# Two products of nothing per pass ahead of the experts, one of them outside the planner's account

## The chip, the cores and the metric

The kernel runs on one core of a Trainium2 chip. The metric is the device time of one execution in microseconds (us); lower is better. A core has five engines that run side by side, each in the order of its own instruction stream: TensorE (PE in the profile; its weight loads are listed as PEld), VectorE (DVE), ScalarE (ACT), GpSimd (POOL) and SyncE (SP), which here issues the transfers. They wait for one another on semaphores. TensorE's clock is granted by a throttle and can be halved for a time; the profile shows what was granted.

## What is computed

Four layers in a row over `x` of 8 sequences, 512 tokens and 128 features, each added to `x` behind a layer norm: a state-space block (a convolution, a scan over the tokens with decay), a mixture of eight experts, a local attention with 16 heads, and the same mixture again.

```python
x = L0_attn_a_x
x = x + _L0_attn_a_ref(_layernorm(x, axis=-1), L0_attn_a_W_in, ...)
x = x + _L0_ffn_ref(_layernorm(x, axis=-1), L0_ffn_w_router, ...)
x = x + _L0_attn_b_ref(_layernorm(x, axis=-1), L0_attn_b_Wq, ...)
x = x + _L0_ffn_ref(_layernorm(x, axis=-1), L0_ffn_w_router, ...)
```

The mixture is dense: every token goes through all eight experts, which are weighted afterwards.

```python
g = jnp.einsum('bsh,ehf->ebsf', x, w_gate)
u = jnp.einsum('bsh,ehf->ebsf', x, w_up)
h = jax.nn.silu(g) * u
expert_out = jnp.einsum('ebsf,efh->ebsh', h, w_down)
...
out = jnp.einsum('ebsh,bse->bsh', expert_out, cw)
```

## The kernel before

Features lie on the 128 partitions, the 512 tokens of a sequence along the free side. Products that need precision are three products of split operands (a high part and a low remainder, `matmul3`). The experts are one long stream, `ffn_stream`: for each of two layers, eight sequences, eight experts and four slices of the hidden width it issues three products for the gate (`g`), three for the up projection (`u`) and, some slices later, three for the down projection (`y`). Between them ACT takes silu of `g`, DVE multiplies by `u`, and two engines split the result `h` into high and low parts. The first sequence of the first layer is done in halves of 256 tokens. State-space and attention work of other sequences is put in beside this stream.

The order of the work is not left to the hardware nor written out by hand. While the program is built, a planner keeps an account of time. `Clock` holds for each engine the end of its last instruction, and books a cost for each new one (`cost`, and `product` for PE). `Engine` wraps a hardware engine: a call on `pe`, `act`, `dve`, `pool` or `sp` issues the real instruction and books it. The work is written as generators in `Lanes`; `tick` gives the next step to the one that can start soonest by the account. What comes out is one fixed order of instructions for each engine. A call on `nc.tensor`, `nc.vector` or another raw engine issues an instruction that the account never hears of.

Before the first experts the front of sequence 0 has to be done: its layer norm (`x_m`, `xn_m`), transposes (`tp_m`), the input projection (`mh`), the convolution (`mv`), the products for step and state inputs (`mde`, `mbc`), spreads of the rows over partitions (`mbx`, `mcx`), the decays (`mdec`) and scans (`mst`), the output products (`mo`), then the experts' layer norm (`xn_f`), transposes (`tp_f`) and the router (`lps_f`, `rps_f`, `cps_f`). All this is short work that goes from engine to engine, on two halves of 256 tokens (`first_halves`). Meanwhile ACT and POOL split the experts' weights (`wg`, `wu`, `wd`) into high and low parts.

During this front the build runs the loop that the change touches, lines 1747 to 1757. `warm` is an accumulator tile of one bank, 128 by 512. Each time no lane has anything to start (`lanes.tick()` did nothing) and the account is past `WARM` = 3.5 us, it issues one product of nothing on PE: weights `sel[:, 0]` (128 by 128), moving operand 256 columns of `sel`, result into the left half of `warm`. Nobody reads that result. The call books its cost by `product`, and the loop then adds 0.1 us to PE's end. It stops when the first half of the experts' input is planned to be there; the bank is freed by `freed(e)`. All warm products write the same tile.

Later, `keep_warm` (line 1766) issues similar products into a bank of their own, tile `idle`, where the experts' stream waits. The change leaves them as they are.

In the profile nearly all instructions carry line 269, the one line of `Engine` that issues them, so they are told apart by the names of their tiles. `warm<-sel` are the products of nothing.

Of the kernel before, what the change touches and what calls it, by code (L numbers as in the profile page):

```python
# [18 lines left out]
P = 128  # L19
B, L, DIM = 8, 512, 128  # L20
NT = L // P
HALF = L // 2
# [355 lines left out]
def block_kernel(ctx: ExitStack, tc: tile.TileContext, x, pack_a, pack_b, pack_c, w_qkv, mask, mask_t, w_o,  # L378
                 w_gate, w_up, w_down, out):
    nc = tc.nc  # L380
# [40 lines left out]
    def take(who, shapes, names):  # L421
        held[who] += len(shapes)
        del lanes.free["bank"][: len(shapes)]
        return [ps.tile(shape, F32, tag="s", name=name) for shape, name in zip(shapes, names)]
# [6 lines left out]
    def side(shape, name):  # L431
        return (yield from sides((shape, name)))[0]

    def freed(t, who="others"):

        held[who] -= 1
        lanes.give("bank", t + TO_PE)
        return t
# [9 lines left out]
    def load_x(b, i, tag):  # L448

        yield from lanes.take("x")  # L450
        if i:
            yield "S", done[b, i]
        t = lnp.tile([P, NT, DIM], F32, tag="x", name=f"x_{tag}", bufs=NX)
        e = sp.dma_start(out=t, in_=xs[b, i].rearrange("(t p) d -> p t d", p=P))
        return t, e
# [6 lines left out]
    def now(gen):  # L462

        try:
            next(gen)
        except StopIteration as stop:
            return stop.value
        raise AssertionError("no buffer is free")
# [636 lines left out]
    def ffn_preps():  # L1105
        for s in range(1, 2 * B):
            k, b = divmod(s, B)
            turn["prep"] = s
            yield lambda: (b, 2 * k + 1) in done and pos[0] >= s - LEAD
            xc = yield from load_x(b, 2 * k + 1, f"f{k}_{b}")  # L1110
            yield from ffn_prep(k, b, xc)
# [291 lines left out]
    def attention_preps():  # L1403
        yield lambda: "weights" in done
        consts = yield from attention_consts()
        for b in range(B):
            yield lambda: (b, 2) in done and (b < 2 or ("heads", b - 2) in done)
            yield from attention_prep(b, consts)
# [310 lines left out]
    with mctx:  # L1719
        sb = msb  # L1720
        mc = {}

        def late(part):
            return lambda: pos[0] >= turn[part] - MAMBA_DUE

        def fronts(seqs):
            for b in seqs:
                turn["front"] = b
                xc = first_x
                if b:  # L1730
                    xc = yield from load_x(b, 0, f"m{b}")
                    yield lambda: ("front", b - 1) in done
                yield from mamba_front(b, sb, mc, xc)
                done["front", b] = 0.0

        def backs(seqs):
            for b in seqs:
                turn["back"] = b
                yield lambda: b in handed and (b - 1, 1) in done
                yield from mamba_back(b, sb, mc, lambda gen: lanes.add(gen, due=late("back")))  # L1740

        first(fronts(range(1)))
        first(mamba_consts(sb, mc))
        lanes.add(ffn_weights(sb))
        clock.hold = INF

        warm = now(side([P, L], "warm"))
        while (0, 0) not in ready or ready[0, 0][1] == 0:
            if lanes.tick():
                continue  # L1750
            if clock.now > WARM:
                sel = mc["sel"]
                e = pe.matmul(warm[:, :HALF], sel[:, 0], sel[:, : HALF // P], start=True, stop=True)
                clock.end["T"] += 0.1
            else:
                clock.now += 0.03
        freed(e)

        done["first"] = 0.0
        lanes.add(backs(range(1, B)), due=late("back"))  # L1760
        lanes.add(fronts(range(1, B)), due=late("front"))
        lanes.add(ffn_preps(), rank=0, due=lambda: pos[0] >= turn["prep"] - PREP_DUE)
        lanes.add(attention_preps(), rank=QRANK, joins=JOIN_ATT)
        stream = ffn_stream()

        def keep_warm():

            if pos[0] < WARM_TO and clock.now > clock.end["T"] + WARM_GAP and lanes.are_free("bank"):
                t, = take("experts", [[P, L]], ["idle"])
                sel = mc["sel"]  # L1770
                freed(pe.matmul(t[:, :HALF], sel[:, 0], sel[:, : HALF // P], start=True, stop=True), "experts")

        while "weights" not in done or (B - 1, 1) not in done:
            if next(stream):
                lanes.idle()
                keep_warm()
            else:
                lanes.tick()
# [63 lines left out]
def build(arrays):  # L1842
    import concourse.bacc as bacc

    nc = bacc.Bacc("TRN2", target_bir_lowering=False, num_devices=1)
    args = [
        nc.dram_tensor(name, a.shape, mybir.dt.from_np(a.dtype), kind="ExternalInput").ap()
        for name, a in arrays.items()
    ]
    args.append(nc.dram_tensor("out", (B, L, DIM), F32, kind="ExternalOutput").ap())  # L1850
    with tile.TileContext(nc) as tc:
        block_kernel(tc, *args)
    return nc
# [10 lines left out]
```

## Time and profile before

| | us |
|---|---|
| median of 3 runs | 1352.26 |
| lowest and highest | 1350.01 and 1354.05 |
| the profiled execution | 1351.71 |
| its span, first to last instruction | 1349.9 |
| PE busy, share of the span | 1328.8, 98% |
| warm products on PE, busy | 17.9 (111 of them) |
| first warm product, last warm product | 2.3 and 32.8 |
| first product of the experts (`g`) | 34.25 |

Times in the trace count from the start of the span. The timeline lists, for each engine, runs of like instructions with start and length and, in brackets, how long the engine had stood idle before them and what ended that idle time. The length of a product is longer than the distance from one to the next, since products overlap in PE's pipeline; so the distance between starts (the pitch) is what a further product costs, not its length.

### The profile page before, as it was taken

The page shows a single profiled execution, that of the slowest core. Times are in us where ns is not written, and L with a number is a line of the kernel's source. Part 1 is how long each engine was busy: PE and PEld are TensorE (multiplying, and loading weights), DVE is VectorE, ACT ScalarE, POOL GpSimd, SP SyncE. Part 2 cuts the span into 40 slices and gives each one's busy share as a digit, 9 for nine tenths or more (in the row PEclk, how much of TensorE's full clock was granted, in tenths as well). Part 3 has the DMA queues.
Part 4 walks back from the last instruction along what each step waited for, and adds up shares of the span by engine and source line. Part 5 has one row for each costly group of instructions (what it writes and reads, how often), then busy time and mean ns, then how long its engine had stood idle before and what let it go on. Part 6 is the DMA issues. An engine that isn't in the chain of part 4 may idle for free.

```text
span 1349.9 us, 29483 instructions
## 1 busy us (share of the span) xinstructions
PE 1328.8 (98%) x10261; PEld 1053.4 (78%) x10261; DVE 1038.5 (77%) x3114; ACT 964.2 (71%) x1694; POOL 941.4 (70%) x1042
## 2 busy tenths in 40 slices
PE   7999999999999999999999999999999999999998
PEld 7877778788788877777777777777777777778886
DVE  6887888688888877897788887888888787845443
ACT  7768576867787556776777777777877767765654
POOL 5877576776767757676766767767677676777776
PEclk9999999999999999999999999999999999999999
DMA  4320303232111261344344453344443434121111
GB/s 126 95 82 28 87 24 101 64 80 76 42 48 56 63 86 52 72 102 113 79 102 114 98 125 88 95 110 102 104 99 96 114 76 102 47 71 53 40 40 40
DMA packets 182204, 107.74 MB, mean 80 GB/s; under 512 B 86401, under 2 KB 162088, under 8 KB 182056
## 3 DMA queue, kind: packets, MB, share of 16 engines
q1 hardware_dynamic: 182056, 105.87, 31.6%
q8 instruction: 81, 1.33, 0.4%
q14 instruction: 67, 0.55, 0.1%
HBM read 77.64 MB, written 27.79 MB: 78 GB/s over the span
## 4 chain that ended last, share of the span: by engine, by line
PE 91%; ACT 2%; issue 2%; POOL 2%; DVE 1%; POOLq 0%; DVEq 0%
PE u L269 26%; PE g L269 25%; PE y L269 25%; PE ao L269 2%; PE aw L269 2%; PE as L269 2%; PE mo L269 1%; POOL h L269 1%; PE aqk L269 1%; ACT h L269 1%; DVE h L269 1%; PE aout L269 1%; PE mde L269 1%; PE yp L269 1%; PE tp_f L269 0%
## 5 line engine op out<-in xcount | busy, mean ns | idle before, releaser
L269 POOL TENSOR_TENSOR h<-h,h 128x512 fp32r<-128x512 f32 x492 | 639.8, 1309 | 280.0 <-ACT h L269 223.2
L269 PE MATMUL u<-xt_f,wu 128*128 128x512 f32 (+1 forms) x1584 | 451.4, 395 | 3.6 <-ACT h L269 2.7
L269 PE MATMUL g<-xt_f,wg 128*128 128x512 f32 (+1 forms) x1584 | 448.4, 393 | 2.1 <-ACT h L269 1.9
L269 PE MATMUL y<-h,wd 128*128 128x512 f32 (+1 forms) x1584 | 445.6, 392 | 1.4 <-POOL h L269 0.8
L269 DVE TENSOR_TENSOR h<-u,h 128x512 f32<-128x512 f32 x420 | 285.8, 686 | 157.7 <-PE u L269 109.8
L269 ACT ACTIVATE h<-g 128x512 f32<-128x512 f32 x512 | 303.4, 597 | 124.8 <-PE g L269 100.6
L269 ACT CAST h<-h 128x512 fp32r<-128x512 f32 x437 | 268.3, 618 | 169.2 <-DVE h L269 167.6
L269 PEld LDWEIGHTS g<-xt_f,wg 128*128 128x128 f32 x1584 | 288.5, 189 | 70.2 <-ACT h L269 3.0
L269 PEld LDWEIGHTS y<-h,wd 128*128 128x128 f32 x1584 | 288.3, 188 | 70.3 <-POOL h L269 1.5
L269 PEld LDWEIGHTS u<-xt_f,wu 128*128 128x128 f32 x1584 | 286.7, 189 | 71.5 <-ACT h L269 4.1
L269 POOL TENSOR_TENSOR acc<-acc,cwb 128x512 f32<-128x512 f32 (+1 forms) x114 | 148.0, 1298 | 52.1 <-DVE cwb L269 44.9
L269 ACT ACT_TABLE_LOAD x109 | 139.8, 1283 | 25.2 <-PE g L269 23.7
L269 DVE CUSTOM_DVE_ANT_0 amasked<-as,maskq 128x60 f32<-128x60 f32 x640 | 95.3, 213 | 4.9 <-PE as L269 4.6
L269 DVE TENSOR_TENSOR cwb<-y,cwb 128x512 f32<-128x512 f32 (+1 forms) x116 | 77.4, 668 | 14.1 <-PE y L269 13.6
L269 DVE TENSOR_TENSOR apt<-aw,maskk 125x400 f32<-125x400 f32 (+2 forms) x160 | 88.1, 570 | 0.0
L269 DVE SCALAR_TENSOR_TENSOR h<-h,g 128x512 f32<-128x512 f32 x92 | 62.3, 681 | 28.3 <-ACT h L269 27.8
L269 ACT ACTIVATE apt<-apt 125x400 f32<-125x400 f32 (+2 forms) x160 | 81.5, 540 | 0.4
L269 DVE SCALAR_TENSOR_TENSOR h<-u,h 128x512 f32<-128x512 f32 x92 | 62.5, 683 | 3.3 <-PE g L269 0.5
L269 DVE DVE_READ_ACCUMULATOR2_ANT amx<- 128x1 f32 x640 | 51.9, 81 | 0.0
L269 DVE CAST h<-h 128x512 fp32r<-128x512 f32 x75 | 50.6, 675 | 1.2
L269 DVE COPY v<-avr 125x128 f32<-125x128 f32 (+2 forms) x40 | 25.5, 638 | 26.5 <-PE ao L269 26.0
L269 PEld LDWEIGHTS ao<-apt,v 125*32 125x32 f32 (+2 forms) x1280 | 27.4, 109 | 14.6 <-DVE h L269 4.0
(205 smaller groups left out, 1241.4 us busy)
## 6 DMA issues: line engine op xcount, KB each, us to landing
cwb<-cwd_f SPq DMA_DIRECT2D x124, 256.0 KB
aqd<-apc SPq DMA_DIRECT2D x32, 192.0 KB
ks<-aqd SPq DMA_DIRECT2D x48, 93.8 KB
x_fo<-x SPq DMA_DIRECT2D x16, 256.0 KB
aqd<-apc SPq DMA_DIRECT2D x32, 128.0 KB
x_f<-x SPq DMA_DIRECT2D x15, 256.0 KB
qs<-aqd SPq DMA_DIRECT2D x48, 75.0 KB
aod<-aos SPq DMA_DIRECT2D x24, 100.0 KB
```

What stands on the lines that cost most here:

```text
L269: f(*args, **kw)
```

## The change

Each pass of the loop issues a second product of nothing. It has the same weights and the same moving operand and writes the right half of `warm`. It is issued on the raw engine, so the account doesn't book it: the planned order of all else is the same.

```diff
             if clock.now > WARM:
                 sel = mc["sel"]
                 e = pe.matmul(warm[:, :HALF], sel[:, 0], sel[:, : HALF // P], start=True, stop=True)
+
+                nc.tensor.matmul(warm[:, HALF:], sel[:, 0], sel[:, : HALF // P], start=True, stop=True)
                 clock.end["T"] += 0.1
             else:
                 clock.now += 0.03
```

## The prediction

> **What bounds the kernel now.** I read the page first: its engine shares and the chain of waits, to see which engine sets the end.
>
> ```profile
> span 1349.9 us, 29483 instructions
> ...
> PE 1328.8 (98%) x10261; PEld 1053.4 (78%) x10261; DVE 1038.5 (77%) x3114; ACT 964.2 (71%) x1694; POOL 941.4 (70%) x1042
> ...
> PE 91%; ACT 2%; issue 2%; POOL 2%; DVE 1%; POOLq 0%; DVEq 0%
> ```
>
> TensorE (PE) is occupied for 98% of the span and carries 91% of the chain that ended last. Almost nothing behind the first 34 us can swallow a late start; whatever PE starts late there, it ends late. So the question is how much later the experts (products g, u, y) begin. Next I read the products of nothing by their tile, and PE's occupied time in the stretches they fill (columns: stretch, us, busy us and count).
>
> ```profile
> L269 PE MATMUL warm<-sel x111: 274/283/579, 2.3 to 32.8; 128*128 128x256 f32 x111
> ...
> 9.72:11.19 1.47, 1.47 (x11) 1.27 (x10) 1.00 1.07 369
> 23.92:24.56 0.64, 0.64 (x3) 0.55 (x3) 0.50 0.00 0
> 28.34:31.34 3.00, 3.00 (x23) 2.79 (x23) 1.00 0.00 0
> ```
>
> There are 111 of them, from 2.3 to 32.8 us. Their pitch at full clock: eleven take 1.47 us, of which the last one's own length is 0.28, so (1.47 - 0.28) / 10 = 0.12 us. At the half clock (the 0.50 column) three take 0.64, 0.21 each. The build's account books 0.22 for each pass of the loop (256 / 2245 + 0.003, and 0.1 on top), so it has long reckoned with PE later than it was; but what counts is the order that came of it, and that the trace shows these runs without a gap between two products.
>
> Third, PE's waits ahead of 34 us and behind it (columns: us in total, times, longest).
>
> ```profile
> PE mbx L269 <- DVE mst L269: 2.6, 1, 2.6
> PE warm L269 <- POOL sel L269: 2.3, 1, 2.3
> PE mbc L269 <- ACT mxb L269: 1.8, 1, 1.8
> PE tp_f L269 <- DVE xn_f L269: 0.4, 1, 0.4
> PE mbx L269 <- DVE mbc L269: 0.2, 1, 0.2
> ...
> PE rps_f L269 <- DVE mcx L269: 0.2, 1, 0.2
> ```
>
> The 2.3 us are the start of PE's work, ahead of every product of nothing. The other five are all the room there is: 5.2 us, four of them ahead of the experts' start, the fifth at 37.5 us.
>
> Last, the clock by stretches (columns: us, then busy time and count of PE, PEld, DVE, ACT, POOL, then granted clock, DMA).
>
> ```profile
> 9.38:12.79 3.41, 1.81 (x12) 1.56 (x12) 2.83 (x5) 2.67 (x7) 3.13 (x4) 1.00 1.09 366
> 19.62:23.03 3.41, 1.13 (x10) 0.93 (x8) 2.59 (x6) 3.31 (x9) 0.00 (x0) 1.00 0.00 0
> 23.03:26.44 3.41, 3.11 (x14) 3.12 (x15) 3.24 (x7) 3.29 (x8) 0.12 (x1) 0.50 0.00 0
> 67.40:70.82 3.42, 2.27 (x8) 1.19 (x8) 3.39 (x11) 3.37 (x5) 0.95 (x2) 1.00 0.01 2
> 70.82:74.23 3.41, 3.41 (x15) 3.02 (x15) 2.50 (x8) 3.40 (x8) 2.65 (x5) 0.50 0.26 77
> 173.22:176.63 3.41, 1.49 (x7) 0.87 (x6) 1.25 (x3) 3.38 (x6) 2.37 (x2) 1.00 0.21 72
> 176.63:180.04 3.41, 3.40 (x8) 2.75 (x9) 2.48 (x4) 2.17 (x4) 1.75 (x2) 0.50 0.01 5
> ```
>
> Three times the clock is halved for 3.41 us, each time behind a stretch of that length with few products in it. These stretches cost up to 1.7 us each (half of 3.41).
>
> **The change, part by part.** Nothing is removed or moved. 111 products are added, each behind its twin: same weights, same 256 columns, the other half of the same accumulator tile, so the pitch of the twin is the nearest row: 0.12 us, taken. Its ends: 0.11 (the pitch of the 128-column mo products at full clock, eight in 1.05 us) and 0.21 (half clock). Nothing cheaper: PE runs its stream in order. The account doesn't see them, so the order of all engines stays. No DMA, no instruction of another engine and no queue is touched. Added work: 111 x 0.12 = 13.3 us on PE.
>
> What of it shows is followed from product to product. "Late" is against before; at each step the later of "PE free" and "operand there" decides.
>
> - wdt_ps, before at 6.39: 19 more products. The first 19 took 4.12 us, about sixteen at 0.21 and the rest at 0.12, so the full clock came at 5.96, where the grid of 3.41 us of the clock rows puts it too. It comes then either way, so the 19 more run at 0.12: late 2.3.
> - tp_m, 7.38: 4 more, late 2.8 (PE). mh, 8.76: 8 more, late 3.7 (PE; its operand, by ACT's and DVE's casts behind tp_m, is late 2.8). mh's third product waited for DVE until 9.38 and no longer does: mh ends at 13.3, late 3.4.
> - ACT's mv, 10.27: before, mh had ended at 9.88 and ACT was still at wxz until 10.25. Now it starts as mh ends, 13.4: late 3.1. This carries on by DVE and ACT to mxb.
> - mbc, 12.99: PE is free at 11.03 + 3.5 + 11 x 0.12 = 15.85, mxb is there at 16.0. Late 3.1, by its operand; the wait of 1.8 is nearly filled.
> - mbx, 15.10: 6 more. PE free at 18.6, operand at 18.2: late 3.5 (PE). From here ACT and DVE (tanh, exponentials, clips, scan mst) run late by 3.5, set by mde just behind.
> - mbx of the second half, 19.41: 5 + 11 = 16 more, late 5.4. Nobody needs it yet; DVE takes it up at 26.8.
> - mbx, 23.33: 8 more. PE free at 20.59 + 5.4 + 0.96 = 26.95; mst is there at 23.28 + 3.5 = 26.8. Late 3.6. The wait of 2.6 is filled, so the clock should not halve here.
> - mcx, 27.06: from the last step on PE has 2 + 6 + 2 + 8 products at 0.12 and eight mo at 0.11, 3.0 us at full clock: free at 30.0. Its bank is freed by DVE (mcx ends at 26.84) at 30.4: late 3.3, by DVE. The clock's gain ends at this wait.
> - tp_f, 31.77: 2 + 23 = 25 more, 3.0 us. PE was free at 31.18, now at 37.5; xn_f (31.63 before, behind DVE and POOL, both late by at most 3.6) is there at 35.2. Late 5.7, PE. This is the term that decides: the 23 had 0.4 us of room.
> - lps_f, 33.02: 7 more, late 6.5. The first g, 34.25, starts at 40.8.
> - rps_f, 37.48: its wait of 0.2 is gone (DVE is late 5.8 by tp_f and lps_f): late 6.3.
>
> So 13.3 are added, 7.0 are hidden: 5.2 in the waits, the rest in what the half clock at 23 us and mh's and mv's waits had cost. Behind 38 us nothing is added, and the waits that remain have POOL, ACT and DVE as their releasers, which are fed by the late PE themselves (POOL waits for the router's pr_f at 39.4, ACT for g, DVE for u). The chain of waits runs unbroken from mo at 37.75 to the end, so its 6.3 us arrive there.
>
> [...]
>
> The profiled execution took 1351.71, its span and 1.8 around it; 1351.71 + 6.3 = 1358.0. The median of the runs shown is 1352.26, 0.55 above it; I stay with the sum.
>
> **The rivals.**
>
> *The clock pays it back (not slower).* The two later halved stretches, at 70.8 and 176.6, follow gaps that straddle the 3.41 us grid in a certain way. 6.3 us is 1.85 stretches, so the gaps fall elsewhere on the grid; if each stretch then holds products for about 40% of it (in the 9.38 row eleven warm and one mh, by their pitches 1.55 us or 45%, kept the clock; in the 19.62 row ten at 0.12, 35%, lost it) both halvings go: 6.3 - 2 x 1.7 = 2.9, giving 1354.6. It decides from 2.3 us saved on, where the change sinks into 0.3%. Against: the gap at 68 to 70.5 is nearly as long as a stretch and will mostly be caught somewhere; the grid need not stand the same in every execution, so before has its lucky runs too. Chance 0.16.
>
> *Weights set the start.* The low parts of the experts' weights are made on POOL (wg, wu, wd), and they are late only by 3.3 to 3.6, from ACT. If they, not PE, release the experts between 40 and 60 us, 3.5 remain: 1355.2. For: the chain up to 30 us names POOL wg, wu, wd. Against: no PE wait on a weight stands among those behind 34 us. Chance 0.06.
>
> *The second product is dearer.* If it can't run at the twin's pitch, 0.21 each: 23.3 added. The waits hold the same 7, so about 16: 1368. For it only the keep-warm "idle" products, which wait for one another at 0.44. Against: those change banks, warm products share one and show no such wait. Chance 0.04.
>
> *It doesn't do what it says:* the second product folds away: 1351.7. Weights are reloaded for each of the 111 now, so nothing is folded in before. Chance 0.02.
>
> **How the numbers follow.** Forecast, 6.3 us in whole: 0.72. The low end is the forecast less both halvings and 0.5 for DVE's smaller lateness, 1354.1. The high end: one more halving (1.7), 0.7 for a clock that opens later in the first 6 us, 0.55 for the median: 1361.0. Weights fall inside, dearer products and folding outside. About 0.3%, 4.06 us on 1352.26, can be told from no change, so slower begins at 1356.3. The forecast's own range is 1356.3 to 1361.0: losing one halving leaves 4.6 us. Slower: the forecast and the dearer case, 0.76. Same: clock, weights, and half of the folding, 0.23. Faster needs 10 us against the sum, which no row offers; the other half of the folding, should the run be a lucky one, 0.01.
>
> **What would show it.** Some 222 warm products, the last near 39 us, pitch 0.12; PE's wait for mst at 23 us gone and the clock full up to 40; its wait for mxb at most 0.3; tp_f ending a warm run without a wait at about 37.5; the first g near 40.8; behind that the same rows as before, shifted. I am wrong if the first g starts before 39 or if PE's waits behind 40 us shrink by more than 1 us; then work that didn't move with PE had been setting them. If g is at 40.8 and the end is not 6 late, look for the half clock.

## The result, and the profile after

| | before | after |
|---|---|---|
| median, us | 1351.61 (6 runs) | 1358.05 (6 runs) |
| lowest and highest, us | 1350.01 and 1354.05 | 1356.93 and 1358.80 |
| profiled execution, us | 1351.71 | 1358.00 |
| its span, us | 1349.9 | 1356.2 |
| warm products | 111 | 222 |
| start of the first g, of rps_f, us | 34.25, 37.48 | 40.57, 43.53 |

The changed kernel takes 1.0047 times as long, with a 95% interval of 1.0034 to 1.0060: 6.4 us by the medians, 6.3 by the two profiled executions.

The page of the changed kernel: its span, the engines and the chain of waits by engine.

```profile
span 1356.2 us, 29705 instructions
...
PE 1339.5 (99%) x10372; PEld 1064.6 (79%) x10372; DVE 1039.3 (77%) x3114; ACT 964.2 (71%) x1694; POOL 941.6 (69%) x1042
...
PE 92%; ACT 2%; POOL 2%; DVE 2%; issue 1%; POOLq 0%; DVEq 0%
```

PE has 111 more products and 10.7 us more of busy time; DVE, ACT and POOL have the same counts and the same work to within 0.8 us. Nothing but PE's stream grew.

The warm products of the changed kernel by their line (the second ones are on 1755), and PE's waits ahead of 41 us (us in total, times, longest).

```profile
L269 PE MATMUL warm<-sel x111: 278/283/582, 2.3 to 38.9; 128*128 128x256 f32 x111
...
L1755 PE MATMUL warm<-sel x111: 278/283/420, 2.7 to 39.0; 128*128 128x256 f32 x111
```

```profile
PE warm L269 <- POOL sel L269: 2.3, 1, 2.3
PE mbc L269 <- ACT mxb L269: 0.6, 1, 0.6
PE g L269 <- DVE lt_f L269: 0.2, 1, 0.2
```

Of the five waits of before, 5.2 us, one of 0.6 is left, and a new one of 0.2 at the first g. PE's timeline at the end of the front (start, length, and in brackets the wait ahead) shows where the lateness comes out:

```profile
37.09 0.28 PE L1755 MATMUL warm<-sel 128*128 128x256 f32 x1
37.21 0.38 PE L269 MATMUL tp_f<-ident,xn_f 128*128 128x128 f32 x2
...
39.19 0.41 PE L269 MATMUL lps_f<-xn_f,route 128*32 128x128 f32 x4
...
40.57 0.62 PE L269 MATMUL g<-xt_f,wg 128*128 128x256 f32 x3 [0.21 <-DVE lt_f L269]
```

tp_f follows the last second product at the pitch of 0.12 and waits for nobody, 5.4 us later than before, where it had waited 0.4 for xn_f. The seven doubled products behind it add the rest.

The clock of the changed kernel by stretches (us, busy time and count of PE, PEld, DVE, ACT, POOL, granted clock, DMA):

```profile
19.62:23.03 3.41, 3.41 (x29) 3.08 (x28) 1.84 (x4) 2.84 (x7) 1.29 (x1) 1.00 0.00 0
23.03:26.44 3.41, 3.41 (x31) 3.41 (x30) 2.39 (x6) 3.31 (x9) 0.00 (x0) 1.00 0.00 0
73.71:77.12 3.41, 2.43 (x9) 1.45 (x10) 3.41 (x15) 3.36 (x5) 0.69 (x2) 1.00 0.01 2
77.12:80.54 3.42, 3.40 (x14) 2.82 (x14) 2.32 (x5) 3.41 (x8) 2.92 (x5) 0.50 0.28 77
179.52:182.94 3.42, 1.49 (x7) 0.92 (x6) 1.27 (x3) 3.39 (x6) 2.16 (x2) 1.00 0.21 71
182.94:186.35 3.41, 3.41 (x9) 2.42 (x8) 2.25 (x4) 1.95 (x4) 2.14 (x2) 0.50 0.02 6
```

The halved stretch at 23 us is gone: PE is busy for the whole 3.41 us from 19.62 on, where before it was busy for 1.13. The two later ones are still there, 6.3 us further on.

### The profile page after: what moved, and what is told of

Read it like the earlier page. It is cut to its first block, busy times and chain, and to the rows that moved or that the text cites. A ratio compares the mean times of both kernels' runs of the same rounds, so it can differ in the third digit from the quotient of the medians.

```text
span 1356.2 us, 29705 instructions
## 1 busy us (share of the span) xinstructions
PE 1339.5 (99%) x10372; PEld 1064.6 (79%) x10372; DVE 1039.3 (77%) x3114; ACT 964.2 (71%) x1694; POOL 941.6 (69%) x1042
## 3 DMA queue, kind: packets, MB, share of 16 engines
q1 hardware_dynamic: 182056, 105.87, 31.9%
## 4 chain that ended last, share of the span: by engine, by line
PE 92%; ACT 2%; POOL 2%; DVE 2%; issue 1%; POOLq 0%; DVEq 0%
PE u L269 26%; PE y L269 25%; PE g L269 25%; PE ao L269 2%; PE aw L269 2%; PE as L269 2%; PE mo L269 1%; POOL h L269 1%; PE warm L269 1%; PE aqk L269 1%; PE warm L1755 1%; ACT h L269 1%; PE mde L269 1%; DVE h L269 1%; PE aout L269 1%
```

## The experiments

Each starts from the kernel before. The diffs show the lines that matter; the counters in them (`n_warm`, `added`) are set to 0 ahead of the loop. The theory: every further product costs PE 0.12 us; it shows where the products of a run end later than the next operand comes, and is hidden where they end sooner; what PE is late at the experts' start it is late at the end. The flat rival: 6.4 us over 111 products, 0.058 each, wherever they stand. Lateness, where it is given, is the start of a product in one trace less its start in the trace of before.

### Where the second products stand

```diff
+                if n_warm < 81:        # >= 81 in the run with the last 30
+                    nc.tensor.matmul(warm[:, HALF:], sel[:, 0], sel[:, : HALF // P], start=True, stop=True)
+                n_warm += 1
```

The first 81 alone:

> A second product only in the first 81 of the 111 passes (all that lie ahead of the mo products at 27.5 us). Theory (0.12 us a product, shown only where PE has no room): the front's operands run 3.6 us late as with the full change, but the run of 23 has its 0.4 us of room back, so tp_f waits for xn_f again and the experts start 3.5 us late: +3.5 us on before. Rival (a flat cost of 6.4 / 111 = 0.058 us for each product, wherever it stands): 81 x 0.058 = +4.7 us. Rival (the clock or the weights, not PE's lateness, made the difference): nothing in particular follows, and PE's late start would not equal the late end.

Measured: 1355.82 against 1352.28, ratio 1.0024 (1.0014 to 1.0035). The last 30 alone:

> A second product only in the last 30 passes (the run of 23 ahead of tp_f and the run of 7 ahead of lps_f). Theory: 23 x 0.12 = 2.8 less the 0.6 between the last warm product's pitch and tp_f gives tp_f 2.2 late, lps_f 3.0, less 0.2 at rps_f: +2.8 us on before; together with the first 81 it makes the 6.3 of the full change. Flat rival: 30 x 0.058 = +1.7 us.

Measured: 1354.02 against 1352.28, ratio 1.0020 (1.0010 to 1.0030). By the medians the first is +3.5, the theory's number, and the second +1.7, the flat rival's. Both intervals hold both numbers (1.9 to 4.7 and 1.4 to 4.1 us; the rival's 4.7 is at the edge), so the times alone don't decide. The traces say more. PE's timeline of the first 81:

```profile
35.67 0.49 PE L269 MATMUL tp_f<-ident,xn_f 128*128 128x128 f32 x2 [0.79 <-DVE xn_f L269]
```

With the run of 23 left single, tp_f waits for xn_f again and is 3.9 late, not 5.4. In the trace of the last 30, tp_f is 3.6 late and rps_f 4.3, of which 1.4 had come before any second product, with the clock:

```profile
19.29:22.70 3.41, 1.46 (x13) 1.25 (x11) 2.28 (x6) 3.28 (x9) 0.00 (x0) 1.00 0.02 5
22.70:29.53 6.83, 6.22 (x29) 6.22 (x30) 5.53 (x11) 6.62 (x14) 3.23 (x3) 0.50 0.00 0
```

Behind the gap at 20 to 23 us the clock was at half here for two stretches. Less the 1.4, the 30 cost 2.9; the theory had 2.8. By the end only 2.0 is left, since the halvings near 70 and 177 us of before are both missing in this execution.

### Products put only where PE waits

```diff
+                for _ in range(1 if 31 <= n_warm < 42 else 2 if 64 <= n_warm < 72 else 0):
+                    nc.tensor.matmul(warm[:, HALF:], sel[:, 0], sel[:, : HALF // P], start=True, stop=True)
+                n_warm += 1
```

> Second products only where PE then waits in before: one in each of the 11 passes ahead of mbc (wait 1.8 us, 1.3 added) and two in each of the 8 passes ahead of the mbx of the second half that waits for mst (wait 2.6 us, 1.9 added). Theory: none of the 27 added products is late for an operand, so the front loses nothing, and the clock is not halved in it, which cost up to 3 us in those executions of before where the grid fell badly: 0 to -2 us on before, -0.5 in the median. Flat rival (0.058 a product): +1.6 us. Each at 0.12, whole: +3.2 us.

Measured: 1351.97 against 1352.21, ratio 1.0002 (0.9993 to 1.0011). 27 products for nothing; the whole 3.2 us lies outside the interval (-0.9 to +1.5 us), the flat rival's 1.6 just outside. PE's waits in the front:

```profile
PE mbc L269 <- ACT mxb L269: 1.3, 1, 1.3
PE tp_f L269 <- DVE xn_f L269: 1.0, 1, 1.0
PE mbx L269 <- DVE mst L269: 0.6, 1, 0.6
```

All three operands still end a wait, so no added product was in anyone's way: the wait for mst shrank from 2.6 to 0.6 us. In the medians the gain that was hoped for from the clock can't be told from nothing. The traces show one in the front and a loss behind it. In this execution the clock opened at 7.47 us, as it did in two runs shown further down whose front is that of before (7.50 and 7.46, products in the dense stream). All three are 1.4 us late at mbc. The two others were then halved twice in the front, and tp_f is 3.0 late there; here it was not halved, and tp_f is still 1.4 late. But the halved stretches at 72 and 178 us came here and were missing in those two, so at 181 us the lateness is 1.4 against 0.8.

### Three products a pass

```diff
+                for _ in range(2):
+                    nc.tensor.matmul(warm[:, HALF:], sel[:, 0], sel[:, : HALF // P], start=True, stop=True)
```

> Three products a pass, two of them outside the account. Theory: the full change has used up the room (PE's waits ahead of 40 us fell from 5.0 to 0.8 us), so the third product shows nearly whole: 13.3 less the 0.6 left at mbc and a little at tp_f and rps_f, about +12.5 on the full change, +18.9 on before. Flat rival: +6.4 on the full change, +12.9 on before.

Measured: 1367.97 against 1352.28, ratio 1.0126 (1.0112 to 1.0140), that is +15.7 by the medians and 15.1 to 18.9 by the interval. The rival's 12.9 is out, the theory's 18.9 is its very edge. In the trace rps_f is 12.1 behind that of the full change, as worked out (12.5). By the end 2.2 of it are gone, 1.5 of them at 183 to 186 us and 0.2 at 77 to 80, where the changed kernel's clock was halved, the rest in small steps; this execution has one halved stretch behind the front, at 88 us, not two.

### Products where PE has no room at all

```diff
+                        if k == 0 and b >= 2 and added[0] < 111:
+                            added[0] += 1
+                            sel = mc["sel"]
+                            nc.tensor.matmul(g[:, :HALF], sel[:, 0], sel[:, : HALF // P], start=True, stop=True)
                         t = products(g, "g")
```

> Before, and 111 products of nothing outside the account, one ahead of each g of the experts from the third sequence of the first layer on, where PE has no room. Theory: each shows whole, 111 x 0.12 = +13.3 us on before (+11.9 if the pitch is the 256 columns alone). Flat rival (0.058 each): +6.4 us.

Measured: 1378.40 against 1351.84, ratio 1.0202 (1.0184 to 1.0220): +26.6, twice the theory's number and four times the rival's. The lateness grows evenly, from 0.8 at 181 us to 13.4 at 487, 0.11 for each product, and then jumps by 12.6 between 487 and 490 us of before. The waits from 480 to 520 us name the cause:

```profile
POOL eye L269 <- PE g L1313: 15.7, 1, 15.7
...
PE as L269 <- DMA ks<-aqd: 11.2, 2, 9.8
```

The attention's tiles take over the memory of sel. POOL's eye, and the clearing of ks behind it in POOL's stream, waited 15.7 us until the last added product had read sel; so the ks transfers came late and PE stood 11.2 us, 9.8 of them in one piece; the clock was at half from 505.9 to 516.1 us. That was of the experiment's own making, and a second one put three products ahead of each g, so that they end early:

```diff
-                        if k == 0 and b >= 2 and added[0] < 111:
+                        for _ in range(3):
+                            if k == 0 and b >= 2 and added[0] < 111:
...
```

> As the run with 111 products in the dense stretch, but three ahead of each g, so that they are over before 290 us, long before the attention's tiles take the place of the weights of nothing. Theory (0.12 whole where PE has no room; the other 13 us of the earlier run came of the attention's tile eye, which waited until the last product of nothing had read sel): +13.0 us on before, and no wait of PE for the ks transfers near 500 us. If each product costs 0.24 there, +26 us again.

Measured: 1363.88 against 1351.99, ratio 1.0089 (1.0075 to 1.0102), +11.9. The lateness goes from 0.8 to 12.7 between 181 and 307 us and stays there to the end. The wait for ks is gone. In the dense stream a product of nothing costs its pitch, about 0.11, whole.

### Fewer products, and none

In both the account still books each one, so the order is that of before.

```diff
-                e = pe.matmul(warm[:, :HALF], sel[:, 0], sel[:, : HALF // P], start=True, stop=True)
+                product = warm[:, :HALF], sel[:, 0], sel[:, : HALF // P]
+                if n_warm % 2 == 0:        # n_warm == 0 in the run with none
+                    nc.tensor.matmul(*product, start=True, stop=True)
+                n_warm += 1
+                e = clock.run("T", "matmul", product[0], product, {}, 0.0, 0.0)
```

> Every other product of nothing left out (56 of 111 remain), account and order as before. Theory: in before the operands, not PE, decide at nearly every step of the front, so nothing is gained by PE being free earlier; what can happen is that the clock opens later or closes again: 0 to +4 us. Flat rival: 55 x 0.058 = -3.2 us.

Measured: 1351.70 against 1351.84, ratio 1.0003 (0.9994 to 1.0013). The rival's -3.2 us is out. In the trace the clock opened at 11.8 us only and was halved twice in the front; rps_f is 0.9 late. The two later halvings are missing in this execution, and at 181 us PE is 1.3 early.

> All products of nothing in the loop but the first are left out, while the account books them, so the order of all else is before's. Theory: PE is never late in the front for their sake, but they kept the clock open; the front's own products run at half clock (about +2 us on the chain by their pitches) and so do the experts' first one or two stretches of 3.41 us (+1.7 to +3.4): +3.5 to +5.5 us on before. Rival (products of nothing are only a burden, so the fewer the better, in line with the change's +6.4): 0 to -1 us.

Measured: 1354.17 against 1351.84, ratio 1.0019 (1.0009 to 1.0029), +2.3. The sign is the theory's, the size is smaller than I had put it. The clock in this trace:

```profile
31.90:38.70 6.80, 5.19 (x20) 3.85 (x21) 5.20 (x10) 1.24 (x3) 5.51 (x6) 0.50 0.17 58
```

It is at half for the first two stretches of the experts (from 31.9 us). It was at half ahead of 28.5 too: the mbx and mo products between 15 and 28 us start 0.21 apart. rps_f is 2.5 late. So by the medians every other product, 56 of them, is worth some 2 us against a single one, the remaining 55 nothing, and the 111 of the change cost 6.4.

### The second product told to the account

```diff
+                e = pe.matmul(warm[:, HALF:], sel[:, 0], sel[:, : HALF // P], start=True, stop=True)
```

> Two products a pass, but the second issued through the planner's wrapper, so that the account books it (0.117 us more a pass). The account then reaches the next step in fewer passes and the products come to about 110 instead of 222. Theory: what cost the time is the number of products in each run on PE, so with the number back the time is before's within 0.3%. Rival (two in a row, or a second half of the bank, is what costs): +3 to +6 us.

Measured: 1356.05 against 1351.84, ratio 1.0029 (1.0019 to 1.0039), +4.2. I had the number wrong: there are 146 products, not 110. A pass books 0.334 us now and booked 0.217 before, so the passes fall only to 73. The number was not back, so neither outcome was put to the test. 35 more at 0.12 would be 4.2, but this trace also has a halved stretch at 17.0 to 20.5 us, so I don't split the sum.

### A narrow second product

```diff
+                nc.tensor.matmul(warm[:, HALF : HALF + 64], sel[:, 0], sel[:, 0, :64], start=True, stop=True)
```

> The second product has 64 columns in place of 256, same weights. It measures what sets the pitch of 0.12. If the columns do, the second costs about 0.03 to 0.06 us, 3 to 7 us in all, nearly all of it inside the 7 us that the full change hid: 0 to +2 us on before. If something that doesn't shrink with the columns does (the weight load that each product brings, or a slower rate for narrow products), the second costs about 0.11 and the time is +5 to +6 us.

Measured: 1363.26 against 1352.28, ratio 1.0079 (1.0065 to 1.0093), +11.0, outside both. At full clock a pair took 0.227, so a quarter of the columns saves 0.01 us. But the clock stayed at half until 21.2 us. With the weights narrowed as well:

```diff
+                nc.tensor.matmul(warm[:64, HALF : HALF + 64], sel[:, 0, :64], sel[:, 0, :64], start=True, stop=True)
```

> The second product has 64 columns and also only 64 columns of weights. In the run with 128 columns of weights the pair took 0.227 us at full clock, so the narrow second cost 0.11. If the weight load sets that, the pair falls to about 0.17 us; if narrow products run at a slower rate of their own, it stays at 0.22. On the time: the earlier run's +11 us came mostly of a clock that stayed at half until 21 us; if the clock again opens so late, +5 to +9 us, if it opens at 6 us as in before, +1 to +3 us.

Measured: 1362.12 against 1351.99, ratio 1.0072 (1.0057 to 1.0088), +10.1, outside both of its ranges too; 1366.91 in the profiled execution. The pair still takes 0.227 at full clock, though the weight loads are shorter, so it isn't the weight load that sets 0.11. Whether it is a slower rate of narrow products or a cost that each product has whatever its width wasn't separated. The clock opened at 32.0 us only. Weight loads, and then the clock rows:

```profile
L269 PEld LDWEIGHTS warm<-sel x111: 187/191/337, 2.3 to 48.4; 128*128 128x128 f32 x111
...
L1754 PEld LDWEIGHTS warm<-sel x111: 133/138/227, 2.5 to 48.5; 128*64 128x64 f32 x111
```

```profile
2.34:16.20 13.86, 13.86 (x63) 13.46 (x64) 4.33 (x18) 5.11 (x13) 4.55 (x8) 1.00 0.97 301
16.20:31.97 15.77, 15.77 (x68) 13.78 (x67) 6.58 (x12) 8.00 (x18) 5.47 (x5) 1.00 0.00 1
```

PE is busy in every moment of both rows. Their clock column says 1.00 only because the record begins with the first grant, at 31.98; the 68 products in 15.77 us, 0.23 each, against 0.12 at full clock, show the half.

### Closing the later gap

```diff
-WARM_TO = 1.5
+WARM_TO = 2.5
```

> Before, with the keep-warm products of the experts' stream allowed for one sequence longer (WARM_TO 2.5 in place of 1.5). They should fill the gap of 1.9 us at 175 us, behind which the clock was halved at 176.6. If that halving goes: -1.7 us on before in those executions that have it, -1 us in the median. Rival (the added products themselves stand in the way, or the planner's order changes for the worse): 0 to +2 us.

Measured: 1355.49 against 1351.99, ratio 1.0026 (1.0016 to 1.0036), +3.5. The halving at 176 us didn't occur in the profiled execution, but the edit didn't do what it was meant to. It added two products there, and the first of them waited for ACT as long as the experts had:

```profile
178.71 0.82 PE L269 MATMUL idle<-sel 128*128 128x256 f32 x2 [1.94 <-ACT h L269]
```

The gap stayed, so what filling it is worth wasn't tested; that no halving followed is no sign of it, since in the run with the first 81 the same wait of 1.94 us passed without one. The planner's order changed (near 200 to 245 us products of the state-space block and of the attention come up to 7 us earlier or 11 later than before). In the trace the clock opened at 11.0 us only, and PE is 2.3 us late behind the front. The median lateness of its products is 0.5 between 310 and 330 us and 5.0 between 400 and 420; between the two lie a new wait of 1.9 us for ACT's h, at 332 us, and a halved stretch at 335. Which of the moved pieces brought that wait was not followed; it stays open. No version beat the kernel before.

## Why the prediction was right

The time was forecast as 1358.0 and is 1358.05; that it is so near is partly luck, since single steps are off by 0.3 us and the clock by more. Lateness by steps, us:

| step | forecast | measured | decided by, in the trace |
|---|---|---|---|
| wdt_ps | 2.3 | 2.0 | PE |
| tp_m | 2.8 | 2.5 | PE |
| mh | 3.7 | 3.5 | PE |
| mv (ACT), first and second | 3.1 | 2.9, 3.3 | mh, then DVE |
| mbc | 3.1 | 3.3 | operand |
| mbx | 3.5 | 3.7 | PE |
| mbx of the second half | 5.4 | 5.5 | PE |
| mbx at 23.33 | 3.6 | 3.7 | PE |
| mcx at 27.06 | 3.3 | 3.0 | PE |
| tp_f | 5.7 | 5.4 | PE |
| lps_f | 6.5 | 6.2 | PE |
| rps_f | 6.3 | 6.1 | PE |
| end, profiled executions | 6.3 | 6.3 | |

- The pitch of 0.12 holds, in the front and, at 0.11 to 0.12, in the dense stream.
- The 0.25 us by which wdt_ps is less late than forecast came of the clock: full from 5.44 us in this execution, 5.96 in that of before.
- At mv I had left out an engine. The second mv product on DVE stood behind DVE's route instructions, which had moved with tp_m and now ended later than ACT's mv: 0.4 us more. So 0.6 of the wait for mxb was left, where I had at most 0.3. A PE that is late also moves what others do beside it.
- At mcx I named the wrong releaser. I took the bank to be freed by DVE's mcx; PE's mcx starts at 30.09, while that instruction runs from 29.76 to 30.45. The scan before it on DVE ends at 29.63 and is what fits. PE was free at 30.1 and went on at once. So the gain from the clock was not lost at a wait there, as I wrote, and the front is more open to the clock than I thought.
- That tp_f decides is shown: left single, the last 30 passes give back the wait of tp_f and 1.5 us of its lateness, 2.2 of that of rps_f.
- That lateness at 38 us arrives at the end is shown by the waits behind 41 us, which are the same in both kernels to 0.1 us each, by the dense runs, and by the traces of the first 81 and last 30, where the lateness changes by more than 0.3 us only at the halved stretches.

The rivals. The clock did not pay it back: both halvings stayed in the profiled execution. Its mean granted clock is 0.997, and so is that of four of the five others (1357.70 to 1358.80 us with it); the sixth has 1.000, so no halved stretch behind the first grant, and took 1356.93, still 5.3 us above the median of before. I had also priced the halvings too high. Where one was missing, lateness fell by 1.5 us at 177 to 180 (first 81: from 3.7 to 2.2) and by 0.7 at 71 to 84 (last 30: from 4.2 to 3.5), 2.2 together and not 3.4. The weights did not set the start: POOL's first low parts behind 26 us are 3.6 late, as I said, but no wait on them came up, and PE's 6.1 went through. The second product was not dearer than its twin, and 222 were executed.

Where I was off is the front's own spread. The dense run with three products has the front of before unchanged, yet its tp_f starts at 34.81, not 31.77:

```profile
34.81 0.49 PE L269 MATMUL tp_f<-ident,xn_f 128*128 128x128 f32 x2
```

```profile
9.38:14.28 4.90, 2.43 (x16) 1.75 (x14) 4.29 (x7) 3.37 (x9) 3.31 (x4) 1.00 1.09 353
14.28:21.11 6.83, 6.73 (x25) 5.24 (x26) 3.34 (x7) 4.92 (x12) 3.38 (x3) 0.50 0.14 39
...
27.94:31.35 3.41, 3.41 (x18) 3.41 (x18) 3.28 (x6) 3.40 (x7) 1.97 (x2) 0.50 0.00 0
```

Here the grid of 3.41 us stands 1.5 us later (an edge at 14.28, not 12.79), the gap ahead of mbc (10 to 14 us) lies in one stretch of it, and behind that the clock is at half for 6.8 us, later again for 3.4. The changed kernel's front is full in its trace from 5.44 us on. So the 6.3 us compare one front with one halved stretch to one with none. Not all of such a difference lasts: in this execution the two later halvings are missing, and of the 3.0 us 0.8 was left at 181 us. How much of the 6.4 us between the medians a different grid would give or take wasn't measured.

## What to carry to other kernels

Work that is put in to keep an engine warm was free here only as long as the next real instruction's operand came later; look at the wait ahead of each real instruction, run by run, before adding more, and put it where there is one: 27 products in front of waits cost nothing here, 30 in front of tp_f and lps_f about 3 us. A planner's account doesn't protect against work that it never hears of, but being heard of doesn't make it free either. With the bounding engine busy 98% of the time, a late start was a late end here, but for the halved stretches, which gave back up to 2.2 us in single executions: it was enough to follow the front, step by step, to get the sum.

## What was not expected of the hardware

- A clock that doesn't open though PE is never idle. With products of 256 and 64 columns in turn it stayed at half until 21.2 us, PE being busy for all of the 18.8 us ahead of that, with narrow weights too until 32.0; in the runs that have 111 or more products of 256 columns and no narrow ones it opened at 5.4 to 7.5 us, once (in the run on the later gap) at 11.0. In the two runs with narrow products PE's busy time as the profile counts it was not enough to open it.
- A product of 64 columns at 0.11 us, against 0.12 for 256, with half the weights or the whole.
- An unchanged front that ran 3.0 us later (tp_f at 34.81, not 31.77) in an execution whose grid stood 1.5 us later, with half clock from 14.28 to 21.11 and from 27.94 to 31.35, where that of before had it from 23.03 to 26.44.
